# A graph network stack: edge scores paced by stage, first score tiles requested in the last sums, and layer 3's bias and transposes moved inside a half block

## The chip, the core and the metric

The kernel runs on one core of a Trainium2 chip. The metric is the time of one execution in device microseconds (us), taken as the median of several runs; lower is better. A core has a matrix engine (TensorE, PE in the profile), three other compute engines (VectorE or DVE, ScalarE or ACT, GpSimd or POOL), SyncE (SP) which here only issues DMA transfers, and 16 DMA engines. Each engine takes its instructions in program order and waits on semaphores for the others.

## The reference

The input x holds 16 images (batch entries) of 1024 nodes with 256 features, in float32; adj is one 1024 x 1024 matrix for all of them, about 1.7% of it nonzero. Four layers follow each other:

```
layer 0:  S[b,u,v] = sigmoid(relu(x_u W1a + x_v W1b + b1) . W2 + b2)
          a[b,v]   = sum_u S[b,u,v] adj[u,v] x[b,u];   m[b,v] = (sum_u adj[u,v] x[b,u]) * x[b,v]
          z = beta1 x + beta2 (a Wa + ba) + beta3 (m Wm + bm)
layer 1:  z = z + relu((adj z) W^T + b)
layers 2, 3:  f = z W1^T;  g = f W2 + b2
          z = softmax_j(leaky_relu(g_i + g_j) + adj[i,j]) f + bias2 + z
```

S counts only where adj is not zero, so the kernel computes the scores of the edges alone.

## The kernel before

**Stages.** The images are worked in four groups of four (GB = 4). A first stage, *free*, needs no edge score: it finds each row's nonzero entries, multiplies every image by the weights of both sides of an edge (`edge_sides`), computes m, and writes the results to HBM. Then each group goes through *edges* (`with_edges`, L1064: the scores as dense 128 x 256 tiles times the projected features) and through two *pairs* of images (`pair_layers`, L1206). A pair has *layer one* (`projected` L1100, `neighbours` L1127), and four *fronts* (L977: the features of an attention layer, and the scale factors from them in `scales`) with eight *sums* (L1035: half a block of 512 target nodes, as eight tiles m of VectorE, L1044, times the features, into four PSUM banks). The functions passed as `finish` end a half block: `second` for layer 2, `third` (L1239) for layer 3, where ScalarE scales the four banks by one over the softmax's total (L1257, reading `share` from L1057), TensorE turns z back (L1251), VectorE adds (L1261), and a DMA writes the output.

**The side work.** The scores are a second stream of instructions, `score_steps` (L704), a Python generator that the main stream pulls along. It has 616 steps: 8 that find indices, and 608 for slots of the row lists, 152 for each group. A slot step gathers 128 rows of 1024 values from HBM (L695, GpSimd, four steps ahead), adds u (L812) and multiplies by W2 after a relu (L814) on VectorE, and sums along four pieces with four ScalarE instructions (L818). At the end of a tile of slots come the sigmoid's pieces (L827 to L831), and then one scatter for each slot (L700, GpSimd) writes the scores into a dense array in HBM. With each new tile ScalarE also prepares the next u (L857). A group's scores are computed while the group before it is in its stages; group 0's in the free stage.

How much of it is laid beside what is set by nominal times: each stage yields the us that it thinks its piece takes, and `Side.along` takes that many steps from the other stream:

```python
def along(self, main, rate=1):
    for us in main:
        self.owed += us * rate
        while self.owed >= 1:
            self.owed -= 1
            next(self.steps, None)
```

RATE (L20) is 0.26 steps per nominal us in the free stage and 0.255 in all others. The tile framework's scheduler may still move instructions against each other. The side's first VectorE instruction of a step is also held back by `paced` (L118) until a recent matmul of the main stream is done.

**The score tiles.** In `with_edges` each of 32 steps loads a tile gd of the dense scores (512 KB, `load_gd` L891, SP's queue, four buffers), lets ScalarE reorder it into gc (L1072, two buffers), and multiplies it with four images' features into all eight PSUM banks. A load waits for all scatters of its group, and for the product 24 before. In group 0 also the exponentials of adj (L1061) and their loads go here. Group 0's first four gd loads are requested ahead, in the free stage (`first_gd`). For the next group `ahead` (L1283) requests the projected features and z during the second pair.

**The end.** In the last group there are no scores left; the second pair's layer one is then partly computed from the row lists (`far_ahead`, L1290).

Of the kernel before, what the change touches and what calls it, by code (L numbers as in the profile page):

```python
# [15 lines left out]
P = 128  # L16

GB = 4
BUFS = 2
RATE = (0.26, 0.255)  # L20
SLOTS = 32
FIRST = 16
EXTRA = SLOTS - FIRST
# [42 lines left out]
def gnn_stack_kernel(  # L66
# [27 lines left out]
    nc = tc.nc  # L94
# [580 lines left out]
    with tc.If(listed > 0) as arm:  # L675
        with ExitStack() as stack:
# [192 lines left out]
            class Side:  # L869
# [2 lines left out]
                def __init__(self, steps):  # L872
                    self.steps, self.owed = steps, 0.0

                def along(self, main, rate=1):
                    for us in main:
                        self.owed += us * rate
                        while self.owed >= 1:
                            self.owed -= 1
                            next(self.steps, None)  # L880
# [30 lines left out]
                return z  # L911

            z_loads = []

            with ExitStack() as first:
                own1 = first.enter_context(tc.tile_pool(name="own1", bufs=1))
# [44 lines left out]
                            clear()  # L961
                        yield us

                side.along(with_zeros(score_free()), RATE[0])
                assert not zeros

            two = stack.enter_context(tc.tile_pool(name="two", bufs=2))
# [8 lines left out]

            def front(x, weights):  # L977

                wT = weights.wT
# [12 lines left out]
                made = {}  # L992
                later.append(lambda: scales(f, weights, made))
                return made
# [36 lines left out]
            def catch_up():  # L1031
                while later:
                    later.pop(0)()

            def sums(made, v, finish):  # L1035

                if "f" not in made:
                    catch_up()
                f, r, ta = made["f"], made["r"], made["ta"]
                cols = slice(v * HN, (v + 1) * HN)  # L1040
                acc = [bank() for _ in range(HT)]
                for jt in range(NT):
                    m = four.tile([P, HN], F32, tag="m", name="m")
                    nc.vector.scalar_tensor_tensor(  # L1044
                        m, r[:, cols], ta[:, jt : jt + 1], ea[:, jt, cols], ALU.max, ALU.mult
                    )
                    for c in range(HT):
                        product(
                            acc[c][:, : D + 1], m[:, c * P : (c + 1) * P], f[:, jt, :],
                            start=jt == 0, stop=jt == NT - 1,  # L1050
                        )
                    if jt == 0:
                        catch_up()
                    yield 1.7
                share = small.tile([P, HT], F32, tag="share", name="share")
                for c in range(HT):
                    nc.vector.reciprocal(share[:, c : c + 1], acc[c][:, D : D + 1])  # L1057
                finish(v, acc, share)
                yield 1.2
# [3 lines left out]

            def with_edges(g, hw, z):  # L1064

                for v in range(N // QN):
                    cols = slice(v * QN, (v + 1) * QN)
                    acc = [[bank() for _ in range(DH)] for _ in range(GB)]
# [30 lines left out]

            def projected(z, keep=None):  # L1100

                y = [node_major("y") for _ in range(2)]
                for jt in range(0, NT, 2):
                    for i in range(2):
# [20 lines left out]
                        nc.vector.tensor_tensor(z[i][:, eh, cols], z[i][:, eh, cols], r, ALU.add)  # L1125

            def neighbours(y, z, cols):  # L1127
                n = cols.stop - cols.start
                acc = [[bank() for _ in range(DH)] for _ in range(2)]
                for jt in range(NT):  # L1130
# [75 lines left out]
            def pair_layers(b, z, ahead, first):  # L1206


                yield from first
# [27 lines left out]


                def third(i):  # L1239
                    def finish(v, acc, share):  # L1240
                        if v == 0:
                            for dh in range(DH):
                                nc.scalar.activation(
                                    z[i][:, dh, :], z[i][:, dh, :], AF.Identity, bias=gat3.bias2[:, dh : dh + 1]
                                )
                        for c in range(0, HT, 2):
                            ps = bank()
                            it = v * HT + c
                            for k in range(2):
                                for dh in range(DH):  # L1250
                                    nc.tensor.transpose(  # L1251
                                        ps[:, k * D + dh * P : k * D + (dh + 1) * P],
                                        z[i][:, dh, (it + k) * P : (it + k + 1) * P], ident,
                                    )
                            st = four.tile([P, 2, D], F32, tag="st", name="st")
                            for k in range(2):
                                nc.scalar.activation(  # L1257
# [7 lines left out]
                    return finish  # L1265


                m0 = yield from front(z[0], gat2)
# [6 lines left out]
                yield from sums(m0, 0, third(0))  # L1275
                m1 = yield from front(z[1], gat3)
                ahead()
                yield from sums(m0, 1, third(0))
                yield from sums(m1, 0, third(1))
                yield from sums(m1, 1, third(1))  # L1280
                assert not later

            def ahead(g):  # L1283
                if g < NGR:
                    loaded.append(([load_hw(g * GB + i) for i in range(GB)], load_z(g)))
                    for load, i in z_loads:
                        load(i)
                    z_loads.clear()

            def far_ahead(z, main):  # L1290

# [8 lines left out]
                        gone += us  # L1300
                        yield us * (0.8 if gone < 68 else 0.61)

                far.along(slots())
                for _ in far.steps:
                    pass
                yield 0

            msg = []
            for g in range(NGR):
                hw, z = loaded.pop(0)  # L1310
                while g not in finished:
                    next(side.steps)
                side.along(with_edges(g, hw, z), RATE[1])
                one = pair_layers(g * GB, z[:2], lambda: None, layer_one(z[:2]))
                if g < NGR - 1:
                    side.along(one, RATE[1])
                    side.along(pair_layers(g * GB + 2, z[2:], lambda: ahead(g + 1), layer_one(z[2:])), RATE[1])
                else:
                    for _ in far_ahead(z[2:], one):
                        pass  # L1320
                    for _ in pair_layers(g * GB + 2, z[2:], lambda: None, from_lists(z[2:], msg)):
                        pass
            assert next(side.steps, "end") == "end"
            psum.pop()
# [129 lines left out]
```

## Time and profile before

| what | value |
|---|---|
| median of 3 runs | 3181.08 us (3177.64 to 3188.89) |
| profiled execution | 3181.81 us, span 3180.1 us |
| granted TensorE clock, mean | 0.994 |
| TensorE busy | 3117.1 us, 98% of the span |
| VectorE, ScalarE, GpSimd busy | 74%, 61%, 57% |
| DMA | 687.48 MB, mean 216 GB/s |
| L818, the scores' sums on ScalarE | 2432 instructions, 407 ns each |
| L812 and L814, the scores on VectorE | 608 each, 1220 and 1219 ns |
| L1072, gd to gc on ScalarE | 128, 2072 ns |
| L695 and L700, gathers and scatters on GpSimd | 1258 and 1261 ns |

The page gives busy times over the whole span; a stage with another limit is seen only in views cut to it. PE rows are matmuls with modelled ends (a float32 product is recorded as two), PEld their weight loads. A row of a timeline has the start in us, the duration, engine, line, operation, output and inputs, how many were merged, and in brackets the idle time before it with what released it. The waits view gives, for each pair of waiting and awaited instruction, the sum in us, how often, and the longest.

### The profile page before, as it was taken

The numbers are of one execution on the slowest core, as the hardware profiler recorded it, in microseconds if no ns is written. First come the engines' busy times: TensorE is split into PE (matmuls) and PEld (weight loads), VectorE is DVE, ScalarE is ACT, GpSimd is POOL, SyncE is SP. The second block draws the span as 40 slices with busy tenths as digits, with TensorE's granted clock in tenths as the row PEclk, the third lists the DMA queues.
The fourth block names the chain that finished last, engine by engine and source line by source line (L and its number), as shares of the span: only waits on it lengthen the run. The fifth ranks groups of instructions, "written<-read, shape, count | busy, mean of one in ns | idle before, by whom it ended". The sixth has DMA issues, their size and how long they took to land.

```text
span 3180.1 us, 39242 instructions
## 1 busy us (share of the span) xinstructions
PE 3117.1 (98%) x12122; PEld 2198.4 (69%) x12122; DVE 2354.2 (74%) x3174; ACT 1946.7 (61%) x6512; POOL 1823.1 (57%) x1483
## 2 busy tenths in 40 slices
PE   8899999999999999999999999999999999999999
PEld 5444554545547768678876866888587688858888
DVE  7797777768775689889777978977798892147844
ACT  3245565656667877567886757788666774513342
POOL 1146778777665666767566665656676652067600
PEclk9999999999999999999999999999999999999999
DMA  9899798788889764766876576587657644476600
GB/s 314 292 324 327 253 304 278 257 256 251 259 284 332 226 185 136 225 189 198 294 240 177 155 205 188 181 294 238 193 142 216 187 133 159 133 253 170 165 7 28
DMA packets 281994, 687.48 MB, mean 216 GB/s; under 512 B 45280, under 2 KB 137440, under 8 KB 274608
## 3 DMA queue, kind: packets, MB, share of 16 engines
q0 software_dynamic: 128224, 387.80, 41.9%
q1 hardware_dynamic: 126112, 245.98, 22.4%
q10 hardware_dynamic: 27440, 51.13, 4.3%
q8 instruction: 97, 1.59, 0.2%
q14 instruction: 121, 0.99, 0.1%
HBM read 553.45 MB, written 131.32 MB: 215 GB/s over the span
## 4 chain that ended last, share of the span: by engine, by line
PE 78%; DVE 8%; DMA 6%; ACT 4%; issue 2%; POOL 1%; SPq 0%; ACTq 0%; DVEq 0%; POOLq 0%
PE bank L126 75%; DMA z<-v_d,slot_v 2%; DVE z L812 2%; ACT z L818 2%; DVE z L814 2%; ACT gc L1072 1%; DVE slot_a L440 1%; DMA gd<-dense_d 1%; PE bank L1227 1%; DVE left L442 1%; DVE m L1044 1%; PE bank L1010 1%; POOL z L695 1%; PE bank L1251 1%; POOL dense_d L700 1%
## 5 line engine op out<-in xcount | busy, mean ns | idle before, releaser
L818 ACT ACTIVATE z<-z 128x256 f32<-128x256 f32 x2432 | 979.9, 407 | 630.0 <-DVE z L814 611.1
L812 DVE TENSOR_TENSOR z<-z,u 128x1024 f32<-128x1024 f32 x608 | 738.6, 1220 | 416.6 <-PE bank L126 305.6
L126 PE MATMUL bank<-feats,m 128*128 128x257 f32 x4096 | 917.1, 381 | 5.2 <-DVE m L1044 4.5
L695 POOL DMA_INDIRECT z<-v_d,slot_v x512 | 644.3, 1258 | 447.0 <-ACT z L818 255.7
L126 PEld LDWEIGHTS bank<-feats,m 128*128 128x128 f32 x4096 | 767.7, 190 | 122.1 <-DVE m L1044 8.0
L700 POOL DMA_INDIRECT dense_d<-gt,slot_at x512 | 645.8, 1261 | 187.2 <-issue 135.8
L814 DVE SCALAR_TENSOR_TENSOR z<-z,w2r 128x1024 f32<-128x1024 f32 x608 | 737.7, 1219 | 9.0
L126 PE MATMUL bank<-gc,hw 128*128 128x256 f32 x2048 | 457.7, 385 | 23.2 <-ACT gc L1072 20.1
L818 ACT ACTIVATION_READ_ACCUMULATOR z<-z 128x1 f32 x2432 | 463.3, 191 | 0.0
L126 PEld LDWEIGHTS bank<-gc,hw 128*128 128x128 f32 x2048 | 389.7, 192 | 90.8 <-ACT gc L1072 30.6
L126 PE MATMUL bank<-adj_sb,h 128*128 128x512 f32 x1024 | 442.4, 592 | 2.8 <-ACT st L322 2.8
L1044 DVE SCALAR_TENSOR_TENSOR m<-rho,tau,adj_sb 128x512 f32<-128x512 f32 x512 | 375.1, 743 | 68.2 <-PE bank L126 65.0
L126 PE MATMUL bank<-adjT_in,y 128*128 128x512 f32 (+1 forms) x960 | 400.5, 578 | 1.5 <-DMA adjT_in<-adjT_d 1.5
L126 PEld LDWEIGHTS bank<-adj_sb,h 128*128 128x128 f32 x1024 | 194.3, 190 | 242.6 <-issue 237.5
L126 PE MATMUL bank<-w,hT 128*128 128x512 f32 (+1 forms) x1024 | 338.0, 491 | 0.0
L126 PEld LDWEIGHTS bank<-adjT_in,y 128*128 128x128 f32 x960 | 182.0, 190 | 215.7 <-issue 201.2
L1072 ACT ACTIVATE gc<-gd 128x1024 f32<-128x1024 f32 x128 | 264.9, 2072 | 94.0 <-PE bank L126 65.8
L126 PEld LDWEIGHTS bank<-w,hT 128*128 128x128 f32 x1024 | 196.6, 193 | 143.1 <-issue 120.8
L126 PE MATMUL bank<-g_wT,z 128*128 128x257 f32 x1024 | 231.1, 380 | 0.2 <-DVE z L1125 0.2
L695 POOL DMA_INDIRECT z<-v_d,x_node x96 | 120.8, 1258 | 176.8 <-ACT z L818 130.9
L126 PEld LDWEIGHTS bank<-g_wT,z 128*128 128x128 f32 x1024 | 191.6, 190 | 30.0 <-issue 2.9
L322 ACT ACTIVATE st<-bank 128x512 f32<-128x512 f32 x128 | 75.8, 592 | 101.2 <-PE bank L126 54.2
(161 smaller groups left out, 2400.7 us busy)
## 6 DMA issues: line engine op xcount, KB each, us to landing
gd<-dense_d SPq DMA_DIRECT2D x128, 512.0 KB, 4.8
dense_d<-zero ACTq DMA_DIRECT2D x64, 512.0 KB, 5.3
adjT_in<-adjT_d SPq DMA_DIRECT2D x112, 256.0 KB, 3.7
h<-in_x_dram SPq DMA_DIRECT2D x19, 1024.0 KB, 12.7
u_d<-st SPq DMA_DIRECT2D x64, 256.0 KB, 5.9
v_d<-st SPq DMA_DIRECT2D x64, 256.0 KB, 6.4
hw_d<-st SPq DMA_DIRECT2D x64, 256.0 KB, 7.0
u<-u_d POOLq DMA_DIRECT2D x32, 512.0 KB, 8.4
```

What stands on the lines that cost most here:

```text
L126: recent.append(nc.tensor.matmul(*args, **kw))
L322: nc.scalar.activation(st[:, c, :2, :], ps.rearrange("p (s k) -> p s k", s=2), AF.Copy)
L440: nc.vector.max(out=slot_a[:, t, s], in_=src)
L442: nc.vector.match_replace(out=left, in_to_replace=slot_a[:, t, s], in_values=src, imm_value=-1.0)
L695: return nc.gpsimd.indirect_dma_start(out=dst, out_offset=None, in_=src[:], in_offset=bass.IndirectOffsetOnAxis(ap=at, axis=0), **how,)
L700: return nc.gpsimd.indirect_dma_start(out=dst[:], out_offset=bass.IndirectOffsetOnAxis(ap=at, axis=0), in_=src, in_offset=None,)
L812: paced(nc.vector.tensor_tensor(z, z, u, ALU.add))
L814: nc.vector.scalar_tensor_tensor(zk, zk, 0.0, w2r[:, None, :].to_broadcast([P, GB, D]), ALU.max, ALU.mult)
L818: nc.scalar.activation(zk[:, c, :], zk[:, c, :], AF.Copy, accum_out=s[:, k, c : c + 1])
L1010: nc.tensor.transpose(ps[:, c * P : (c + 1) * P], f[:, jt, D : D + 1].to_broadcast([P, P]), ident)
L1044: nc.vector.scalar_tensor_tensor(m, r[:, cols], ta[:, jt : jt + 1], ea[:, jt, cols], ALU.max, ALU.mult)
L1072: paced(nc.scalar.activation(gc, gd.rearrange("p n i -> p i n"), AF.Copy), 16)
```

## The change

The change has four parts. The rate becomes a table by stage, where each stage names itself in `doing[0]`: 0.225 instead of 0.255 in the edges, 0.288 in layer one, as before elsewhere. A call `soon`, ahead of the last sums of a group's second pair, requests the next group's first four gd tiles if that group's scores are finished (all its scatters put into the program). Layer 3's bias pass over z goes from the end of an image's first half block to its third m tile. And each half block's eight transposes of z go from its end to its last two m tiles, four with each, so that two PSUM banks are taken there already.

```diff
-RATE = (0.26, 0.255)
+PACE = dict(free=0.26, edges=0.225, one=0.288, fronts=0.255, sums=0.255)
...
-                def along(self, main, rate=1):
+                def along(self, main, pace=PACE):
                     for us in main:
-                        self.owed += us * rate
+                        self.owed += us * pace[doing[0]]
...
-            def sums(made, v, finish):
-
+            def sums(made, v, finish, early=None):
+
+                doing[0] = "sums"
...
                     if jt == 0:
                         catch_up()
+                    if early:
+                        early(v, jt)
                     yield 1.7
...
                 def third(i):
-                    def finish(v, acc, share):
-                        if v == 0:
+                    turned_back = []
+
+                    def early(v, jt):
+                        if v == 0 and jt == 2:
                             for dh in range(DH):
                                 nc.scalar.activation(
                                     z[i][:, dh, :], z[i][:, dh, :], AF.Identity, bias=gat3.bias2[:, dh : dh + 1]
                                 )
+                        if jt < NT - 2:
+                            return
+                        ps = bank()
+                        for k in range(2):
+                            it = v * HT + (jt - NT + 2) * 2 + k
+                            for dh in range(DH):
+                                nc.tensor.transpose(
+                                    ps[:, k * D + dh * P : k * D + (dh + 1) * P],
+                                    z[i][:, dh, it * P : (it + 1) * P], ident,
+                                )
+                        turned_back.append(ps)
+
+                    def finish(v, acc, share):
                         for c in range(0, HT, 2):
-                            ps = bank()
+                            ps = turned_back.pop(0)
                             it = v * HT + c
-                            for k in range(2):
-                                for dh in range(DH):
-                                    nc.tensor.transpose(
...
-                yield from sums(m0, 1, third(0))
-                yield from sums(m1, 0, third(1))
-                yield from sums(m1, 1, third(1))
+                yield from sums(m0, 1, *t0)
+                yield from sums(m1, 0, *t1)
+                soon()
+                yield from sums(m1, 1, *t1)
...
+            def soon(g):
+
+                if g in finished:
+                    first_gd.extend(load_gd(g, 0, ut) for ut in range(4))
```

`soon` loads with `load_gd`'s own default, six products back instead of 24. `front`, `with_edges`, `projected` and `neighbours` set `doing[0]` in the same way, and the last group's `far_ahead` keeps its own rate.

More of the change, by code (lines that the diff above doesn't have):

```diff
@@ L913, in gnn_stack_kernel @@
             z_loads = []
+            doing = ["free"]
             with ExitStack() as first:
@@ L962, in with_zeros @@
                         yield us
-                side.along(with_zeros(score_free()), RATE[0])
+                side.along(with_zeros(score_free()))
                 assert not zeros
@@ L977, in front @@
             def front(x, weights):
+                doing[0] = "fronts"
                 wT = weights.wT
@@ L1064, in with_edges @@
             def with_edges(g, hw, z):
+                doing[0] = "edges"
                 for v in range(N // QN):
@@ L1100, in projected @@
             def projected(z, keep=None):
+                doing[0] = "one"
                 y = [node_major("y") for _ in range(2)]
@@ L1127, in neighbours @@
             def neighbours(y, z, cols):
+                doing[0] = "one"
                 n = cols.stop - cols.start
@@ L1204, in from_lists, with pair_layers @@
                     onto(z, slice(t0 * P, t0 * P + n), lambda i, eh: turned_back[i, eh][:, :n])
-            def pair_layers(b, z, ahead, first):
+            def pair_layers(b, z, ahead, soon, first):
                 yield from first
@@ L1245, in finish @@
                                 )
+                        if jt < NT - 2:
[10 more added lines that the diff above has]
+                    def finish(v, acc, share):
                         for c in range(0, HT, 2):
-                            ps = bank()
+                            ps = turned_back.pop(0)
                             it = v * HT + c
-                            for k in range(2):
-                                for dh in range(DH):
[L1251 to L1254, printed above, removed]
                             st = four.tile([P, 2, D], F32, tag="st", name="st")
@@ L1264, in finish @@
                             )
-                    return finish
+                    return finish, early
                 m0 = yield from front(z[0], gat2)
@@ L1274, in pair_layers @@
                 yield from sums(m1, 1, second(1))
-                yield from sums(m0, 0, third(0))
+                t0, t1 = third(0), third(1)
+                yield from sums(m0, 0, *t0)
                 m1 = yield from front(z[1], gat3)
                 ahead()
-                yield from sums(m0, 1, third(0))
-                yield from sums(m1, 0, third(1))
-                yield from sums(m1, 1, third(1))
+                yield from sums(m0, 1, *t0)
+                yield from sums(m1, 0, *t1)
+                soon()
+                yield from sums(m1, 1, *t1)
                 assert not later
@@ L1301, in slots @@
                         yield us * (0.8 if gone < 68 else 0.61)
-                far.along(slots())
+                far.along(slots(), dict.fromkeys(PACE, 1))
                 for _ in far.steps:
@@ L1306, in far_ahead, with nothing @@
                 yield 0
+            def nothing():
+                pass
             msg = []
@@ L1312, in gnn_stack_kernel @@
                     next(side.steps)
-                side.along(with_edges(g, hw, z), RATE[1])
-                one = pair_layers(g * GB, z[:2], lambda: None, layer_one(z[:2]))
+                side.along(with_edges(g, hw, z))
+                one = pair_layers(g * GB, z[:2], nothing, nothing, layer_one(z[:2]))
                 if g < NGR - 1:
-                    side.along(one, RATE[1])
-                    side.along(pair_layers(g * GB + 2, z[2:], lambda: ahead(g + 1), layer_one(z[2:])), RATE[1])
+                    side.along(one)
+                    last = pair_layers(
+                        g * GB + 2, z[2:], lambda: ahead(g + 1), lambda: soon(g + 1), layer_one(z[2:])
+                    )
+                    side.along(last)
                 else:
@@ L1320, in gnn_stack_kernel @@
                         pass
-                    for _ in pair_layers(g * GB + 2, z[2:], lambda: None, from_lists(z[2:], msg)):
+                    for _ in pair_layers(g * GB + 2, z[2:], nothing, nothing, from_lists(z[2:], msg)):
                         pass
```

## The prediction

> **What bounds the kernel now.** I read the page first: engine shares and the chain that ended last.
>
> ```profile
> PE 3117.1 (98%) x12122; PEld 2198.4 (69%) x12122; DVE 2354.2 (74%) x3174; ACT 1946.7 (61%) x6512; POOL 1823.1 (57%) x1483
> PE 78%; DVE 8%; DMA 6%; ACT 4%; issue 2%; POOL 1%; SPq 0%; ACTq 0%; DVEq 0%; POOLq 0%
> ```
>
> TensorE (PE) sets the end, and the change gives it no less work: its matmuls and transposes are the same, some in another place. So only what its stages take beyond their own matmuls can be won. I cut the span into stages at the first matmul of each kind, in TensorE's timeline.
>
> ```profile
> 1526.46 1.89 PE L126 MATMUL bank<-gc,hw 128*128 128x256 f32 x8
> 1528.88 9.22 PE L126 MATMUL bank<-gc,hw 128*128 128x256 f32 x40 [0.52 <-ACT st L1257]
> 1540.62 83.63 PE L126 MATMUL bank<-gc,hw 128*128 128x256 f32 x384 [2.52 <-ACT gc L1072]
> 1624.87 17.95 PE L126 MATMUL bank<-gc,hw 128*128 128x256 f32 x80 [0.63 <-ACT gc L1072]
> 1642.66 13.98 PE L126 MATMUL bank<-l1wT,z 128*128 128x256 f32 x64
> ...
> 1849.01 1.04 PE L1251 MATMUL bank<-ident,z 128*128 128x128 f32 x8
> 1852.41 15.80 PE L126 MATMUL bank<-feats,m 128*128 128x257 f32 x64 [2.36 <-DVE m L1044]
> ...
> 2652.32 1.04 PE L1251 MATMUL bank<-ident,z 128*128 128x128 f32 x8
> 2658.12 2.08 PE L126 MATMUL bank<-gc,hw 128*128 128x256 f32 x4 [4.76 <-ACT gc L1072]
> 2660.40 110.93 PE L126 MATMUL bank<-gc,hw 128*128 128x256 f32 x508 [0.20 <-ACT st L1257]
> ```
>
> The l1wT row gives the pace of an undisturbed 256-column matmul: 13.8 us to the next stage over 64 is 0.216 us. An edges stage has 512 of them, 110.6 us. The four stages take 127.3 (956.2 to 1083.5), 116.2, 118.9 (2090.4 to 2209.3) and 113.05 us: 16.7, 5.6, 8.3 and 2.5 over, and 4.8 us idle stand before the last. Layer one is at its floor (68.8 us against 68.7). The two-layer part of a pair (fronts and sums) takes 150.3 us in the last two pairs, which have no scores beside them, and 152.7, 152.7, 157.4, 152.5, 154 and 152.4 us in the others: some 20 us over in all.
>
> Then the busy times by stage, same columns as the page, (x) counts instructions:
>
> ```profile
> core 0: us, PE busy (x) PEld busy (x) DVE busy (x) ACT busy (x) POOL busy (x), PEclk, DMA share, GB/s
> 956.00:1083.00 127.00, 116.95 (x511) 97.54 (x510) 68.51 (x80) 107.67 (x227) 62.92 (x52) 0.97 0.88 305
> 1083.00:1152.00 69.00, 69.00 (x196) 36.90 (x195) 50.67 (x54) 40.41 (x163) 44.72 (x37) 1.00 0.70 203
> 1374.00:1526.00 152.00, 151.49 (x736) 129.63 (x735) 143.97 (x213) 116.07 (x415) 108.44 (x76) 1.00 0.63 193
> 1526.00:1642.50 116.50, 112.76 (x518) 96.55 (x517) 81.35 (x98) 110.13 (x265) 74.67 (x63) 1.00 0.88 288
> 2653.20:2771.00 117.80, 112.83 (x514) 98.42 (x513) 14.54 (x33) 67.00 (x36) 0.53 (x1) 0.97 0.49 159
> ```
>
> In the edges (rows 1, 4) ScalarE (ACT) is busy 110 of 116 us; in the last group, without scores, 67. In layer one (row 2) it is busy 40 of 69, VectorE (DVE) 51. In fronts and sums (row 3) VectorE is full. So scores beside the edges cost TensorE time, and beside layer one they don't.
>
> **The pace.** The nominal times that the stages yield, times the rate, give score steps: edges 108.8 (89.6 in group 0) times 0.255, 27.7 (22.8), become 24.5 (20.2) at 0.225; layer one, 68 times 0.255, 17.3, becomes 19.6 at 0.288. The trace agrees: L818 alone has 184, 224 and 232 records in the three edges stages, 8 to a step: 23, 28 and 29 steps. A step holds ScalarE for 1.60 us (four L818, start to start), a gc copy for 2.0.
> Group 0: from 1019 to 1072 ScalarE has no pause (gc, scores and the exponentials of L1061), and TensorE idles 6.3 us before its gc matmuls there (0.79, 0.78, 0.74, 0.51 and 3.52). 2.6 steps fewer free 4.2 us. I take -4 (bounds 0 and -6).
> Group 1: ScalarE loses 3.2 steps, 5.1 us; TensorE idles 3.7 us in the rows above. The 2.52 comes from two score steps and a u tile standing between the second pair of gc copies; in the built order of the changed program single steps stand there. But the last half block's evacuations (L1257) stand behind one step more. I take -3 (-5 to 0).
> Group 2: idle 1.1, 1.4, 1.1, 0.6 and 0.2, and in the new order two steps still stand ahead of its fourth gc. -3 (-6 to 0).
> Layer one gets 2.3 steps more, six times: VectorE 2.3 x 2.44 = 5.6 us, 56 of 69; GpSimd (POOL), with its pauses the fullest, some 4.6 more indirect DMAs of 1.26 us and 0.3 us between two: 42 x 1.56 = 65 of 69. I take 0: VectorE and ScalarE hide it, and TensorE waits only for their pieces at the stage's ends. If GpSimd falls behind, late gathers hold VectorE in front of L1125: up to 1 us each, +6. Nor is a gain excluded, since fewer steps are then owed to the sums; 0 is the near end because the row shows no idle time.
>
> **The first score tiles.** Four gd loads (512 KB each) go to SP's queue before the last sums instead of some 10 us before the edges. In groups 1 and 2 they were issued at 1515.3 and 2080.3, 10 us ahead, and no matmul of theirs waited for one: 0. Behind them on SP stand one z load, wanted at the end of the edges' first quarter (28 us later), and the later gd loads. In group 3 they wait for scatters:
>
> ```profile
> 2626.24 0.97 POOL L700 DMA_INDIRECT dense_d<-gt,slot_at  x1 [21.54 <-DVE gt L831]
> ...
> 2650.03 0.97 POOL L700 DMA_INDIRECT dense_d<-gt,slot_at  x1 [0.30 <-issue]
> ```
> ```profile
> SPq L894 <- DMA dense_d<-gt,slot_at: 28.1, 4, 20.9
> ```
>
> The last score tile's 16 scatters run from 2626 to 2651, loads follow at 2652.3, gc at 2656.1, TensorE at 2658.1. An early request alone would change nothing here; the pace does. By the code's step count 616 steps are due; at the start of this group's second pair 569 are done now, 571 after. Layer one then takes 17.3 or 19.6, and 29.7 or 25.4 remain at 0.255: 116 or 100 nominal us. So the last step, and the scatters, end some 16 us earlier, near 2635, and the loads (4.8 us to land) can be there by 2643, ten before the edges. That takes away the 4.8 us idle. If the scatters stay late, 0.
>
> Here the clock row meets a rule. The granted clock fell to half for 6.8 us around this gap, and for 3.4 us at 1853, after 2.4 us idle. The Trainium skill (TensorE: Matmul & The Clock Gate, Part 1: The HAM clock gate) halves the clock after a window of some 3.4 us idle. By the rule the 4.8 us gap costs its length plus half of the busy part of the slow stretch, 4.4 us: 7.0 in all, and the 2.4 us gap no clock; by the row the latter does too, so small gaps count. The stage's own excess of 2.5 us is mostly the slow start. I take -6.5 (-7.3 to 0).
>
> **Bias and transposes.** 256 transposes of 0.11 us and 32 bias passes of 1.1 us on ScalarE are as many as before. No row has L1251 waiting for the bias pass, so its move wins 0 (if it came late instead, 1.1 us an image, +18; it is placed four tiles ahead, 7 us). In the built order four of a half block's eight transposes now precede its last four matmuls, four follow. What I charge is cover. Before, 8 transposes (0.87 us) and two matmul groups (0.87) stood between the last product and the first matmul that needs an evacuated bank; after, 0.44 + 0.87 = 1.31. A rule speaks against this: the skill (PSUM — Partial Sum Buffer, Specifications (TRN2)) gives 8 banks per partition; four sums, two transpose banks and four new sums are ten, so by the rule every boundary waits for two evacuations, 32 x 0.43 = +14 if none is early. By the trace, the first L1257 ended 0.09, 0.09, 1.42, 1.89, 0.82, 0.73, 1.55, 1.34, 1.72, 1.20, 1.67 and -0.20 us after the last product at the twelve boundaries that lead straight to other sums beside scores: beyond 1.31 six of them, 1.7 us together. I take the row, +2 (below nothing to -5, as the 2.36 us stall at 1852, where m stands behind the output additions, may go; +8 for new ones).
>
> **Sum.** -4 -3 -3 +0 -6.5 +2 = -14.5 us. The profiled execution took 3181.8 (span 3180.1 and 1.7 around it): 3167.3; against the median of 3181.1, 3166.6. I say 3167.
>
> **Rivals.** *As summed*, 0.6, with its own range 3160 to 3171.5. *Half is given back*, 0.25: ScalarE stays the wait in the edges (it is still some 93% busy), and only half of their 10 us and the group 3 gap are won, and the boundaries cost 5: -5 -6.5 +5 is 3175. For it speaks that two steps still stand together in group 2; against it, layer one's idle engines. *The sums become quieter too*, 0.1: the 1852 stall with its clock (4.4 us) and part of the small ones go: -23, 3158. *Slower*, 0.05: at the half-block boundaries the evacuation stands behind one more score step (1.6 us) with nothing to cover it; 24 boundaries have scores beside them. From 0.6 us each it eats the 14.5, from 1.0 the kernel is slower by over 0.3%; at 1.2, +29 in place of the +2: 3194. The trace shows such waits at two or three of 24. *The change doesn't do what it says*: the early request is skipped if the next group isn't finished; the step count has it finished each time. Part of the second case.
>
> About 0.3% (9.5 us) is what a measurement of this kernel can tell from no change. Faster by more (under 3171.5): 0.68; within: 0.26; slower: 0.06. The range 3156 to 3177 leaves the slower case and the tails of the others out.
>
> **What would show it.** ScalarE in the edges of groups 1 and 2 near 104 of 114 us with 24 or 25 steps; those stages at 113 to 115 us and group 0's at 123; group 3's first gc matmul within 0.5 us of the last transposes, clock at full; layer one still 68.8. Wrong if layer one grows past 69.5, if the pairs' sums grow past 154 us, or if the gd loads of group 3 still wait for scatters until 2650.

## The result and the profile after

The changed kernel takes 3157.72 us (median of 6 runs, 3154.12 to 3165.59), against 3179.36 us (6 runs, 3173.95 to 3188.89) for the kernel before on the same chip: a ratio of 0.9932, 95% interval [0.9913, 0.9952]. The profiled execution took 3160.95 us, 20.9 less than the one before. The prediction was 3167, with a range of 3156 to 3177: sign and range held (1.7 us inside the range's near end), and in the profiled executions the gain was 6.4 us larger than the sum (20.9 against 14.5).

The first view is the page: busy times, and the shares of the chain that ended last.

```profile
PE 3110.1 (98%) x12122; PEld 2192.8 (69%) x12122; DVE 2357.7 (75%) x3174; ACT 1949.7 (62%) x6512; POOL 1866.2 (59%) x1483
PE 77%; DVE 8%; DMA 6%; ACT 5%; issue 3%; POOL 1%; SPq 0%; ACTq 0%; POOLq 0%; DVEq 0%
```

All instruction counts of TensorE, VectorE, ScalarE and GpSimd are as before. PE's busy time is 7.0 us shorter with the same matmuls, which fits fewer of them at the halved clock. The page shows no more than that: the kernel still hangs on TensorE, and what changed is where TensorE stands still. So the second view is its timeline, at the places that were shown of before (L1264 are the transposes of z that were L1251, L128 the products that were L126).

```profile
1523.16 1.89 PE L128 MATMUL bank<-gc,hw 128*128 128x256 f32 x8
1525.56 107.31 PE L128 MATMUL bank<-gc,hw 128*128 128x256 f32 x488 [0.50 <-ACT st L1276]
1633.92 3.72 PE L128 MATMUL bank<-gc,hw 128*128 128x256 f32 x16 [1.04 <-ACT gc L1080]
1637.47 2.75 PE L128 MATMUL bank<-l1wT,z 128*128 128x256 f32 x12
...
1843.77 0.60 PE L1264 MATMUL bank<-ident,z 128*128 128x128 f32 x4
1844.21 12.94 PE L128 MATMUL bank<-feats,m 128*128 128x257 f32 x56
...
1922.56 7.13 PE L128 MATMUL bank<-adjT_in,y 128*128 128x512 f32 x16 [0.92 <-DMA adjT_in<-adjT_d]
...
2639.96 0.60 PE L1264 MATMUL bank<-ident,z 128*128 128x128 f32 x4
2640.40 110.67 PE L128 MATMUL bank<-gc,hw 128*128 128x256 f32 x512
```

In group 1's edges the waits are 0.50 and 1.04 us where there were 0.52, 2.52 and 0.63. The 2.36 us that stood behind the transposes at 1852 are gone (1844). Group 3's first gc product follows its transposes at once (2640.40), and its 512 matmuls run without a pause. New is 0.92 us at 1922 in layer one, behind a load of adjT. Cut at the first matmul of each kind, the stages are:

| stage | before, us | after, us | difference | predicted |
|---|---|---|---|---|
| edges, group 0 | 127.3 | 122.3 | -5.0 | -4 |
| edges, group 1 | 116.2 | 114.3 | -1.9 | -3 |
| edges, group 2 | 118.9 | 115.2 | -3.7 | -3 |
| pause ahead of group 3, and its edges | 4.9 + 113.05 | 0 + 110.5 | -7.5 | -6.5 |
| layer one, six scored pairs, in sum | 412.8 | 415.0 | +2.2 | 0 |
| fronts and sums, six scored pairs, in sum | 921.8 | 916.6 | -5.2 | +2 |

(In the sixth pair of before, two matmuls of layer one run ahead of the last sums; they are counted with layer one.) That makes -21.1; the free stage (+0.8) and the last group's layer one (-0.2) leave it within 0.5 us of the span's -20.9. The third view is the busy time in the same stages (columns as on the page; rows: edges 0, layer one, fronts and sums, edges 1, edges 3).

```profile
core 0: us, PE busy (x) PEld busy (x) DVE busy (x) ACT busy (x) POOL busy (x), PEclk, DMA share, GB/s
957.00:1079.30 122.30, 115.00 (x513) 97.20 (x512) 63.29 (x78) 103.07 (x208) 52.17 (x44) 0.99 0.88 302
1079.30:1148.00 68.70, 68.70 (x193) 36.48 (x193) 54.50 (x54) 43.45 (x180) 52.82 (x42) 1.00 0.74 219
1370.60:1523.20 152.60, 152.17 (x742) 130.22 (x741) 144.89 (x216) 117.46 (x421) 112.60 (x79) 1.00 0.65 201
1523.20:1637.50 114.30, 112.63 (x515) 96.16 (x514) 73.59 (x90) 105.09 (x240) 68.54 (x58) 1.00 0.84 273
2640.40:2750.90 110.50, 110.50 (x514) 97.28 (x513) 14.38 (x34) 62.26 (x32) 0.53 (x1) 1.00 0.48 150
```

ScalarE in group 1's edges went from 110.1 to 105.1 us, GpSimd in layer one from 44.7 to 52.8: the side work moved as the table of paces says. In the three edges stages the L820 records (the scores' sums, before L818) are 166, 200 and 205, 21, 25 and 26 steps for 23, 28 and 29. The clock of the last row is full. Fourth, the timeline of GpSimd and SP's queue where group 2 ends, and the waits view's entry for the score tiles (sum, times, longest):

```profile
2618.20 1.43 POOL L702 DMA_INDIRECT dense_d<-gt,slot_at  x1 [0.30 <-issue]
2622.80 1.75 SPq L896 DMA_DIRECT2D gd<-dense_d  x4
```
```profile
SPq L896 <- DMA dense_d<-gt,slot_at: 9.2, 4, 4.3
```

The last scatter now ends 20.8 us before group 2's sums are over, where it ended 2.4 us before that (2651.0 and 2653.4), and all four loads go out together 17.6 us ahead of the edges. The wait for scatters fell from 28.1 to 9.2 us.

### The profile page after: what moved, and what is told of

Read it like the earlier page. It is cut to its first block, busy times and chain, and to the rows that moved or that the text cites. A ratio compares the mean times of both kernels' runs of the same rounds, so it can differ in the third digit from the quotient of the medians.

```text
span 3159.2 us, 39229 instructions
## 1 busy us (share of the span) xinstructions
PE 3110.1 (98%) x12122; PEld 2192.8 (69%) x12122; DVE 2357.7 (75%) x3174; ACT 1949.7 (62%) x6512; POOL 1866.2 (59%) x1483
## 4 chain that ended last, share of the span: by engine, by line
PE 77%; DVE 8%; DMA 6%; ACT 5%; issue 3%; POOL 1%; SPq 0%; ACTq 0%; POOLq 0%; DVEq 0%
PE bank L128 73%; ACT z L820 2%; DVE z L814 2%; DVE z L816 2%; ACT gc L1080 1%; DVE slot_a L442 1%; DMA gd<-dense_d 1%; PE bank L1237 1%; DVE left L444 1%; DMA hw_d<-st 1%; DMA z<-v_d,slot_v 1%; PE bank L1014 1%; POOL dense_d L702 1%; DVE m L1049 1%; POOL z L697 1%
## 5 line engine op out<-in xcount | busy, mean ns | idle before, releaser
L820 ACT ACTIVATE z<-z 128x256 f32<-128x256 f32 x2432 | 979.7, 406 | 604.9 <-DVE z L816 571.5
L128 PE MATMUL bank<-feats,m 128*128 128x257 f32 x4096 | 918.6, 381 | 1.5 <-ACT st L1276 0.6
L697 POOL DMA_INDIRECT z<-v_d,slot_v x512 | 653.8, 1277 | 408.7 <-ACT z L820 229.9
L128 PEld LDWEIGHTS bank<-feats,m 128*128 128x128 f32 x4096 | 764.5, 190 | 115.1 <-DVE m L1049 5.5
L702 POOL DMA_INDIRECT dense_d<-gt,slot_at x512 | 670.4, 1309 | 194.6 <-issue 133.7
L128 PE MATMUL bank<-gc,hw 128*128 128x256 f32 x2048 | 451.7, 382 | 11.3 <-ACT gc L1080 10.3
L820 ACT ACTIVATION_READ_ACCUMULATOR z<-z 128x1 f32 x2432 | 461.5, 190 | 0.0
L128 PE MATMUL bank<-adj_sb,h 128*128 128x512 f32 x1024 | 442.7, 593 | 2.6 <-ACT st L324 2.6
L128 PEld LDWEIGHTS bank<-gc,hw 128*128 128x128 f32 x2048 | 386.6, 190 | 76.0 <-ACT gc L1080 21.6
L128 PE MATMUL bank<-adjT_in,y 128*128 128x512 f32 (+1 forms) x960 | 401.4, 579 | 2.6 <-DMA adjT_in<-adjT_d 2.4
L128 PEld LDWEIGHTS bank<-adj_sb,h 128*128 128x128 f32 x1024 | 194.5, 190 | 243.0 <-issue 237.4
L128 PE MATMUL bank<-w,hT 128*128 128x512 f32 (+1 forms) x1024 | 337.5, 490 | 0.0
L128 PEld LDWEIGHTS bank<-adjT_in,y 128*128 128x128 f32 x960 | 181.7, 190 | 218.0 <-issue 198.9
L128 PEld LDWEIGHTS bank<-w,hT 128*128 128x128 f32 x1024 | 196.2, 192 | 143.7 <-issue 119.7
L128 PE MATMUL bank<-g_wT,z 128*128 128x257 f32 x1024 | 231.8, 380 | 1.3 <-ACT st L1276 1.2
L128 PEld LDWEIGHTS bank<-g_wT,z 128*128 128x128 f32 x1024 | 191.6, 190 | 31.9 <-issue 3.1
L697 POOL DMA_INDIRECT z<-v_d,x_node x96 | 129.4, 1348 | 137.7 <-ACT z L820 83.0
```

The lines of the kernel that those rows point to most:

```text
L128: recent.append(nc.tensor.matmul(*args, **kw))
L697: return nc.gpsimd.indirect_dma_start(out=dst, out_offset=None, in_=src[:], in_offset=bass.IndirectOffsetOnAxis(ap=at, axis=0), **how,)
L702: return nc.gpsimd.indirect_dma_start(out=dst[:], out_offset=bass.IndirectOffsetOnAxis(ap=at, axis=0), in_=src, in_offset=None,)
L820: nc.scalar.activation(zk[:, c, :], zk[:, c, :], AF.Copy, accum_out=s[:, k, c : c + 1])
```

## The experiments

Twelve runs on three other chips. The kernels of one chip share the runs of the kernel before there; its medians were 3206.64, 3198.60 and 3214.44 us (second, third and fourth chip). The kernel before was profiled on the first chip alone. Single profiles on the others hold stray pauses of TensorE of some us, so totals are read from the timed ratios, and a profile only where one stage differs by more or where several profiles agree. Us that stand beside a ratio are its share of the median of before; the difference of the medians is up to 4 us away from that.

**Second chip: the parts by themselves.** The paces without the two other parts: bias pass and transposes back at the half block's end, no `soon`.

```diff
-                soon()
...
-                    def early(v, jt):
-                        if v == 0 and jt == 2:
+                    early = None
+                    def finish(v, acc, share):
+                        if v == 0:
...
-                            ps = turned_back.pop(0)
+                            ps = bank()
+                            for k in range(2):
+                                for dh in range(DH):
+                                    nc.tensor.transpose(
...
```

> The table of paces alone: no early request, bias and transposes at the end of a half block as before. Theory (the pace frees ScalarE in the edges and lets the scatters of the last scored group end some 16 us earlier): the edges stages shrink from 127.3, 116.2, 118.9 and 113.05 us to about 122, 114, 115 and 110.5, and group 3's first gc matmul follows the last transposes within 0.5 us, though nothing is requested earlier, because the loads' own place, 24 products back, is some 10 us ahead: 15 to 18 us less than before, 0.9945. Rival (the early request is what closes group 3's gap): 2 to 5 us of it stay idle, and the gain is 9 to 13 us. Second rival (the sums' gain of 5 us comes from the move inside the half block): the stall of 2.4 us at the end of the first half block of group 1's third image pair, and its slow clock, come back; then 4 to 5 us less gain than the full change.

Measured: 0.9946 [0.9931, 0.9962], 17.3 us of 3206.6, and 13.3 us between the medians. The paces' terms of the prediction (-4 -3 -3 -6.5) hold in sum, and group 3 starts without a pause although nothing is requested early: the first rival fell. But TensorE waited 5.1 us ahead of group 2's edges in this profile, which before did not show. On the second rival, the pause that stood at 1852, see below.

The early request alone has the paces of before and the end as above:

```diff
-PACE = dict(free=0.26, edges=0.225, one=0.288, fronts=0.255, sums=0.255)
+PACE = dict(free=0.26, edges=0.255, one=0.255, fronts=0.255, sums=0.255)
```

> The early request of a group's first four score tiles alone, old paces, bias and transposes as before. Theory: the loads of group 3 still wait for scatters that end at about 2651 us, so its gap of 4.8 us and the slow clock stay, and groups 1 and 2 did not wait for their loads: within 2 us of before, ratio 0.9995 to 1.0005. Rival (the request closes the gap): 5 to 7 us less, 0.998.

Measured: 0.9998 [0.9988, 1.0008]. Its timeline where group 3 starts:

```profile
2669.11 0.97 POOL L702 DMA_INDIRECT dense_d<-gt,slot_at  x1 [0.30 <-issue]
2671.35 1.74 SPq L896 DMA_DIRECT2D gd<-dense_d  x4
2675.28 3.93 ACT L1080 ACTIVATE gc<-gd 128x1024 f32<-128x1024 f32 x2 [17.74 <-DMA gd<-dense_d]
2677.34 1.22 PE L128 MATMUL bank<-gc,hw 128*128 128x256 f32 x2 [4.92 <-ACT gc L1080]
```

The four loads are in one row, asked for early, yet they leave only after the last scatter, and TensorE waits 4.92 us as it waited 4.76. A request can't be earlier than its data: this step of the prediction is shown.

The move inside alone keeps the old paces, without `soon`:

> Bias pass and transposes inside the half block alone, old paces, no early request. The prediction's step: less cover at the boundaries, +2 us (0 to +4), stages other than fronts and sums as before. Rival (the sums' gain of 5 us in the full change comes from here): the six scored pairs' fronts and sums take 5 us less together, and the stall before 1852 us goes, ratio 0.998.

Measured: 1.0015 [1.0001, 1.0030], 4.8 us of 3206.6 lost. The interval only just leaves out no change. The move by itself wins nothing, and its cost is small. The profiles of the second chip also say what moved the pause of 1852. The rows are those of the request alone (old paces, end as before), the move alone (old paces, new end) and the paces alone (new paces, end as before):

```profile
1860.04 14.12 PE L128 MATMUL bank<-feats,m 128*128 128x257 f32 x64 [2.36 <-DVE m L1049]
1858.21 12.41 PE L128 MATMUL bank<-feats,m 128*128 128x257 f32 x56 [3.14 <-DVE m L1049]
1794.41 8.94 PE L128 MATMUL bank<-feats,m 128*128 128x257 f32 x40 [2.36 <-DVE m L1049]
```

In the first two it stands 142.4 and 143.5 us into the fronts and sums of this pair, as it did on the first chip (140.9). In the third nothing stands there any more, and a wait for m has come up 79.2 us into the stage. So the new paces take the pause away from its place, and the move does not. But the stage gets no shorter on these chips: 156.8 us with the paces alone, 157.3 with the request alone. The seven profiles on other chips that have both paces of the change all hold a pause of 1.4 to 2.4 us at 78 to 79 us and take 156.8 to 157.5 us; only the profile of the change on the first chip has none and takes 153.4.

Paces and early request together, the end as before:

> Full change without the move inside the half block. Theory (the move wins nothing by itself): within 2 us of the full change, some 20 us less than before, edges and group 3's start as in the full change. Rival (the move brings 5 us in the sums): 15 to 16 us less than before, with the six scored pairs' fronts and sums at some 918 us in all, as before, and not at 914.

Measured: 0.9922 [0.9907, 0.9936], 25 us of 3206.6, and 21 us between the medians: nearer to the theory's 20 than to the rival's 15 to 16. The request, worth nothing alone, adds 0.24% (7.7 us) to the paces.

**Third chip: which pace, and the cover.** The change as it is:

> The full change once more, as the reference for the other kernels of this series on their chip. Theory (the pace carries the gain, the request adds to it only where score tiles land late, the move inside the half block costs 0 to 4 us): 0.992 to 0.9935 of before. Rival (the move gains 5 us once the pace is changed): 0.9905 or less.

Measured: 0.9967 [0.9956, 0.9978]. The same kernel had 0.9932 on the first chip and the intervals do not meet, and it is also less than was expected here: the gain is not the same on every chip. Its profile has one pause of 7.9 us at the half-block boundary at 2629, in group 2's last pair.

Layer one's pace alone (`edges=0.255, one=0.288`, no request, the end as before):

> Only layer one's pace is raised to 0.288, edges at 0.255, no request, bias and transposes as before. Theory (a gap at group 3's start is a matter of when the last step comes): the last step comes some 40 us earlier, so group 3's scatters are done long before its edges, the gap of 4.8 us and the slow clock go, and the edges of groups 0 to 2 stay at some 127, 117 and 119 us: 6 to 9 us less, 0.9975. Rival (what counts is ScalarE in the edges alone): 0 to 2 us less, 0.9995.

Measured: 1.0002 [0.9994, 1.0011]: the theory missed, and the number is the rival's. Group 3's pause and slow start are gone in the profile (0 and 110.5 us), so the mechanism is there, but one pair's fronts and sums took 162.7 us and group 2's edges 123.7, and nothing is left.

The edges' pace alone (`edges=0.225, one=0.255`):

> Only the edges' pace is lowered to 0.225, layer one at 0.255, no request, bias and transposes as before. One step is then still owed when group 3 is due and is forced there. Theory: the edges of groups 0 to 2 get 9 to 11 us shorter, but the last 16 scatters, the load and the copy of group 3 start only at the end of the last sums, so that TensorE waits some 33 us instead of 4.8: 16 to 20 us more than before, 1.0055. Rival (scatters of the last tile do not hold group 3's loads): 9 to 11 us less than before, 0.9968.

Measured: 1.0045 [1.0031, 1.0059]. The three edges stages take 123.3, 118.4 and 115.8 us, as short as in the change but for group 1, and group 3 pays for it:

```profile
2647.00 0.93 PE L1263 MATMUL bank<-ident,z 128*128 128x128 f32 x7
2681.99 8.29 PE L128 MATMUL bank<-gc,hw 128*128 128x256 f32 x23 [34.06 <-ACT gc L1080]
```

The steps taken from the edges have to be done elsewhere: if they are not, TensorE waits 34 us for score tiles whose scatters come late. So the two paces are one change: each alone gives nothing or loses.

The cover at the boundary taken away: each half block's transposes one m tile earlier, so that none stands behind the last products.

```diff
-                        if jt < NT - 2:
+                        if not NT - 3 <= jt < NT - 1:
...
-                            it = v * HT + (jt - NT + 2) * 2 + k
+                            it = v * HT + (jt - NT + 3) * 2 + k
```

> Full change, with the eight transposes another m tile earlier (in the sixth and seventh of eight), so that none of them stands between the last product of a half block and the next one's matmuls. Theory of the prediction (transposes there cover the wait for evacuated banks): the next half block's third matmul comes 0.87 us after the last product instead of 1.31, and 2 to 5 us more than the full change are lost at the boundaries. Rival (the cover is worth nothing, ScalarE evacuates in time or the order of m tiles decides): within 1 us of the full change.

Measured: 0.9992 [0.9979, 1.0005], 0.25% or 8 us above the change on the same chip. Moving the transposes forward by one more m tile costs more than the 2 to 5 us expected. That the missing 0.44 us of cover is the reason is not shown: TensorE's waits for evacuated banks (releaser ACT st L1276, from the edges on) come to 10.7 us in this profile and to 10.7 in that of the change on the same chip, eight times in each; without the one long pause that both have near 2630 they are 4.0 and 2.8, which makes 1.2 of the 8 us. The PSUM banks are also taken earlier, and other steps stand beside the boundaries; no run tells these apart.

**Fourth chip: is the move inside worth having, and do further paces win?** The change as it is, again:

> The changed kernel as it is, beside variants without its third part on one chip. Theory: the gain is between the two ratios seen so far (0.9932 and 0.9967), near 0.995, and the kernel is slower than the same without the inside move (next run) by 0.1 to 0.4% (3 to 12 us), since the move alone cost 0.15% and taking the cover away changed the boundaries. Rival: the move gains once the pace is changed, and this one is the faster of the two by over 0.1%. Or the difference stays within 0.1% and the different ratios so far were the chips.

Measured: 0.9948 [0.9932, 0.9965], median 3196.61 us.

> The paces and the early request, with bias pass and z transposes at the half block's end as before. Theory: ratio near 0.992, 0.1 to 0.4% under the full change on the same chip. Rival (the inside move gains): above the full change. If the 0.9922 seen before was the mark of its chip, the two agree within 0.1%.

Measured: 0.9911 [0.9894, 0.9928], median 3189.64 us. The intervals do not meet: without the move inside the kernel is faster, by 0.37% in the ratios and 7.0 us in the medians. This version beats both kernels on the chip where all three ran. The single profiles can't show where: this version's happened to be one of its longer executions (span 3198.9 us, for 3190.3 of the change).

> The paces only. On another chip the early request was worth 0.24% on top of the paces (0.9946 against 0.9922), with score tiles that came late. Theory: the request again adds 0.1 to 0.3%, so the ratio here is near 0.994. Rival (the prediction's): the request adds nothing once the last group's tiles are written in time, and this run agrees with the one that has the request within 0.1%.

Measured: 0.9937 [0.9917, 0.9957]. The request again adds 0.26% (8.4 us) to the paces. On either chip the two intervals overlap at their ends; that sign and size agree on both is what speaks for it. The profiles show what it meets, and why before did not: the start of group 2's edges with the paces alone (SP's requests, ScalarE's copy, TensorE), and below it the same requests and copy in the move alone, which has the old paces, on the second chip.

```profile
2083.80 0.32 SPq L910 DMA_DIRECT2D z<-zb_d  x1
2084.62 15.28 SPq L896 DMA_DIRECT2D gd<-dense_d  x4
2096.27 2.00 ACT L1080 ACTIVATE gc<-gd 128x1024 f32<-128x1024 f32 x1 [7.94 <-DMA gd<-dense_d]
2098.32 2.07 PE L128 MATMUL bank<-gc,hw 128*128 128x256 f32 x4 [3.82 <-ACT gc L1080]
```
```profile
2085.51 7.46 SPq L896 DMA_DIRECT2D gd<-dense_d  x3
2089.52 2.11 ACT L1080 ACTIVATE gc<-gd 128x1024 f32<-128x1024 f32 x1
```

From issue to the copy 11.65 us pass in the first, 4.0 in the second (2085.51 to 2089.52), and 4.0 in the trace of before on the first chip (2080.3 to 2084.27). The lead is the same ten us, and it isn't the chip: the second chip has 4.0 us with the old paces and 13.1 us (2085.97 to 2099.04) with the paces alone. (On the third chip, old order, it is 4.7 us with the edges' pace alone and 7.1 with layer one's.) What differs is the order on SP's queue. With the paces alone a load of z, 1 MB, leaves 0.7 to 0.8 us ahead of the score tiles; in before and in the move alone the last z load leaves 20 us ahead, and the next one behind three tiles. With the request the tiles go out 18 us ahead, in front of that z load, and no version with paces and request has a pause at this start. That the z load is the cause fits these profiles; it was not tested by itself.

Yet this start does not explain the gain. In both profiles with paces and request (end as before) a pause stands later in the same stage, 7.33 us at 2118 and 4.85 at 2126, and group 2's edges with their pauses take 126.2 and 124.8 us, for 125.1 and 124.2 with the paces alone. It is group 1's edges that are shorter there, 113.1 and 113.5 us for 120.9 and 116.9. Where the 0.25% of the timed runs lies is open.

Edges slower still and layer one faster, with the request and the end as before:

```diff
-PACE = dict(free=0.26, edges=0.225, one=0.288, fronts=0.255, sums=0.255)
+PACE = dict(free=0.26, edges=0.21, one=0.30, fronts=0.255, sums=0.255)
```

> Paces and request, with the edges slower still (0.21 for 0.225) and layer one faster (0.30 for 0.288), bias and transposes at the end. 1.4 to 1.6 score steps fewer in each edges stage, one more in each layer one. Theory: ScalarE still is the wait in edges 0 (123 us, floor 110.6), so edges gain 1 to 2 us each, layer one gives 0 to 1 us back six times: between 4 us faster and 3 us slower than with the change's paces, most likely 1 us faster. Rival: layer one is at its limit (it already grew by 2.2 us in sum), and grows by more than the edges gain: slower by 3 us or more.

Measured: 0.9964 [0.9947, 0.9981], 13 us above the change's paces by the medians. The rival's sign held and its place did not: in the profiles layer one takes 415 us in sum against 419, the edges 353.6 against 359.6, and only the fronts and sums grow, 941 against 929. That makes 2 of the 13 us; a single profile does not hold the rest. That other score steps meet the half blocks there is my reading, and is not shown. Going further in the same direction loses; between and beyond nothing was tried.

**What the stray pauses are.** On the first chip TensorE's pauses over 0.4 us in fronts and sums (from 1150 us on) come to 4.0 us before and 1.2 after; on the other chips they come to 7.6 to 25.0. The longest, 4.7 to 7.9 us at one boundary near 2630, is in three profiles with the move inside, the paces and the request (the change on the third and fourth chip, and the version without cover). None of the five with changed paces for both stages and the end as before has it (the paces alone and with the request, twice each, and the further paces), and the change on the first chip has not either. Timeline of GpSimd and VectorE there, the change on the fourth chip:

```profile
2623.68 0.96 POOL L702 DMA_INDIRECT dense_d<-gt,slot_at  x1 [0.30 <-issue]
2624.63 0.75 DVE L1049 SCALAR_TENSOR_TENSOR m<-rho,tau,adj_sb 128x512 f32<-128x512 f32 x1 [2.10 <-PE bank L128]
2624.95 1.28 POOL L702 DMA_INDIRECT dense_d<-gt,slot_at  x1 [0.30 <-issue]
2626.53 0.97 POOL L702 DMA_INDIRECT dense_d<-gt,slot_at  x1 [0.31 <-issue]
2627.49 0.75 DVE L1049 SCALAR_TENSOR_TENSOR m<-rho,tau,adj_sb 128x512 f32<-128x512 f32 x1 [2.11 <-PE bank L128]
2627.80 1.28 POOL L702 DMA_INDIRECT dense_d<-gt,slot_at  x1 [0.30 <-issue]
2629.39 0.97 POOL L702 DMA_INDIRECT dense_d<-gt,slot_at  x1 [0.30 <-issue]
2630.33 0.23 DVE L1064 RECIPROCAL share<-bank 128x1 f32<-128x1 f32 x2 [2.08 <-remote]
```

and the change on the first chip at the same step of the program:

```profile
2605.08 0.75 DVE L1049 SCALAR_TENSOR_TENSOR m<-rho,tau,adj_sb 128x512 f32<-128x512 f32 x1 [1.05 <-PE bank L128]
2605.18 1.50 POOL L702 DMA_INDIRECT dense_d<-gt,slot_at  x1 [0.30 <-issue]
2606.75 0.75 DVE L1049 SCALAR_TENSOR_TENSOR m<-rho,tau,adj_sb 128x512 f32<-128x512 f32 x1 [0.91 <-PE bank L128]
2606.98 1.36 POOL L702 DMA_INDIRECT dense_d<-gt,slot_at  x1 [0.30 <-issue]
```

In the second fence the two engines alternate: VectorE makes a tile each 1.7 us, as TensorE uses them, and the scatter beside it grows from 0.97 to 1.4 or 1.5 us. In the first, each VectorE instruction starts within 0.05 us of the end of a scatter (2623.68 + 0.96 is 2624.64; 2626.53 + 0.97 is 2627.50; 2629.39 + 0.97 is 2630.36), and only at every second one: a tile takes 2.86 us, the four tiles of lead are used up, and the reciprocals that free the banks come 4 us after the last product (2626.3). The releaser in the bracket is then misleading: the named product had long been done. The Trainium skill (SBUF — State Buffer, SBUF: two separate sides) has a cause that fits: VectorE with two operands in SBUF and a GpSimd instruction that reads SBUF take a shared port as an exclusive lock, and the loser blocks for the whole instruction. The stretched scatters and the delayed tiles are what such a lock would show on either side. But the longest of these pauses, the 7.9 us of the third chip, speaks against it as the only cause (its last scatter, and VectorE's m tiles around it):

```profile
2631.43 0.75 DVE L1049 SCALAR_TENSOR_TENSOR m<-rho,tau,adj_sb 128x512 f32<-128x512 f32 x1 [6.21 <-remote]
2632.15 0.97 POOL L702 DMA_INDIRECT dense_d<-gt,slot_at  x1 [0.30 <-issue]
2635.65 0.75 DVE L1049 SCALAR_TENSOR_TENSOR m<-rho,tau,adj_sb 128x512 f32<-128x512 f32 x1 [3.46 <-remote]
```

There no scatter is stretched, and VectorE stays idle for 2.5 us after the last of them has ended (2632.15 + 0.97 is 2633.12). So the lock is argued from two timelines and contradicted by a third; no experiment thinned the scatters out, and the cause of these pauses is open.

## Why the prediction was right, and where its sum was off

**Edges: right.** -4 -3 -3 was the sum, -10.6 was measured, each group inside its bounds. ScalarE at 105 of 114 us with 25 and 26 steps is the sign that the prediction asked for, and on another chip the edges' pace alone shortens groups 0 and 2 (123.3 and 115.8 us, for 127.6 and 123.7 with the old edges' pace there), though not group 1 (118.4 for 116.2).

**Group 3's start: right.** -6.5 was the sum and -7.5 was measured, 0.2 past its bound. Three runs take it apart as the prediction did: the request alone leaves 4.9 us (gain 0), the paces alone remove the pause, and layer one's pace alone suffices for it. Against the end of the sums the last scatter comes 18 us earlier, for 16 by the step count. The slow clock went with the pause, and the whole stage is at 110.5.

**The early request in groups 1 and 2: 0 was taken, and that step failed elsewhere.** "They were issued 10 us ahead, and no matmul of theirs waited for one: 0" read the landing time, 4 us, off the queue of the kernel before. With the new paces a z load stands ahead of group 2's tiles; on two other chips they then took 13.1 and 11.7 us, TensorE waited 5.1 and 3.8 us at the start, and the request was worth 7.7 and 8.4 us on top of the paces. What it brings on the first chip can't be told from one profile.

**Layer one: 0 was taken, +2.2 measured**, inside its bounds (0 to +6 for late work). The prediction's own mark, 69.5 us, was passed once (69.93). The cause is not the one that was named: the one wait over 0.4 us there is for an adjT load on SP (0.92 us at 1922), not for VectorE behind late gathers. The median landing time of these loads went from 3.6 to 3.8 us and the longest from 9.2 to 12.4; that denser gathers slow them fits, and no run isolates it.

**Fronts and sums: the term that was off.** +2 was the sum, -5.2 was measured, just past the near bound of -5, and this is where the 6.4 us come from. 4.1 of the 5.2 are the pause at 1852 with its slow clock, which was named as what might go and was given to the third rival; with 3157.7 the result lies at that rival's 3158. The pause went with the paces, as the profiles of the second chip show, so the step that failed is the one that set its possible end down to the bias and transposes, and took it at nothing. That it brought 4 us is luck: on the other chips a wait of 1.4 to 2.4 us at another place of the same stage takes back what it gives, and only the first chip's profile has neither.

The bias and transposes do not deserve the 5.2. What the +2 stood for, TensorE waiting for evacuated banks inside the fronts and sums, went from none over 0.4 us to two (0.55 and 0.62 us): 1.2 us, near the 2. But the move as a whole cost more in the timed runs of other chips, 0.15% alone and 0.37% (7 to 12 us) on top of the paces and the request. The sign of the +2 was right; what the rest of that cost is has not been shown.

**The other rivals.** "Half is given back" (3175) fell on the first chip, though on the third the change won only 0.33%, 10.5 us. Over the three chips the ratios 0.9932, 0.9967 and 0.9948 lie on both sides of the 0.9954 that 14.5 us make. The slower case fell on all three chips that ran the full change: the highest upper end of its intervals is 0.9978.

**What stays open.** Why one chip gives 0.9932 and another 0.9967 for the same two kernels: the profiles of the change differ most in the wait of group 1's third pair and in the pause near 2630, and what brings either on was not isolated. Whether the boundary near 2630 is the whole price of the move inside is open too: three profiles with it and five without agree with it, one with it (the first chip) does not.

## What to carry to other kernels

When a side stream is paced beside a main one, take its steps from the stage whose in-order engine is full and give them to one that has room in the same change: either half alone won nothing or lost. Ask before a request is moved up whether its data exist by then. A landing time read off a trace holds for the order of the queue in that trace: when a change shifts the steps, ask which loads will stand ahead of which. A wait that a change removes in one profile may only have moved; look for it in other executions before it is counted as won. And test a part that is expected to cost, as the move off the block's end here, apart from the parts that win.

## What the runs showed of the hardware

The same 512 KB load, issued some ten us ahead of its use, was ready after 4.0 us on the first chip and on the second, and after 13.1 and 11.7 us on the second and fourth where a 1 MB load had left the same queue 0.7 to 0.8 us before it. A scatter's issue on GpSimd took 0.97 us alone and 1.36 to 1.50 us beside VectorE's m tiles in the change on the first chip; on the fourth a tile came only every 2.86 us instead of 1.7, and TensorE lost 4.7 us at that boundary. An idle stretch of TensorE of 2.36 us was followed by 3.4 us of half clock in the trace of before; one of the same length at another place (the paces alone, second chip) by none.
